# Placing two heads' sums in the last graph layer: TensorE transposes against VectorE block transposes and on-chip transfers

## The chip, the cores and the metric

The kernel runs on one core of a Trainium2 chip. A core has TensorE (PE in the profile, with its weight loads as PEld), VectorE (DVE), ScalarE (ACT), GpSimd (POOL) and SyncE (SP), which issues transfers; ACT and GpSimd can issue them too. Work in fast memory lies in SBUF (128 partitions), sums of matmuls in PSUM, and large arrays in DRAM. The metric is the device time of one execution in microseconds.

## The reference

Four graph layers follow one another on 3327 nodes with 512 features. Each is added to its input and normalised by rows. Layers 0, 2 and 3 are attention layers, layer 1 averages over the first 64 neighbours. The last layer, which the change touches, is this (4 heads of 128 features):

```python
h = (x @ W).reshape(N, HEADS, HEAD_DIM).transpose(1, 0, 2)
si = jnp.einsum('hnd,d->hn', h, a1)
sj = jnp.einsum('hnd,d->hn', h, a2)
e = si[:, :, None] + sj[:, None, :]
e = jnp.where(e > 0, e, ALPHA * e)
e = jnp.where(adj[None, :, :] > 0, e, NEG_INF)
attn = jax.nn.softmax(e, axis=-1)
h_prime = jnp.einsum('hij,hjd->hid', attn, h)
...
x = _layernorm(x + jax.nn.elu(h_prime), axis=-1)
```

## The kernel before, in words

Nodes are padded to 26 tiles of 128 (`NT`), in two halves of 13 (`HALF`, 1664 nodes, `IW`). An attention layer runs over the two halves of the receiving nodes and, within each, over four slices of 128 features (`s`; in the last layer a slice is a head). One such pass is a call of `unit`. It walks over the 26 tiles `j` of sending nodes: VectorE makes the weights `t` (L405, 128 x 1664), ACT makes `y` from them (L408), TensorE adds `t` times the features `vj` into four PSUM banks `po` (L428), and a little later adds the rows' denominators into `pd` (L380). The features come by `vj` loads on SP (L416), two tiles to a load, in four buffers; `t` has three buffers.

At the end of a unit `po` holds the head's sums with features on partitions and nodes along the row, and they have to be turned round. The kernel has two ways.

In the last layer's first half (`by_dma`), VectorE transposes each bank in 32 x 32 blocks into `ob` (L446), and four transfers on SP place the blocks in DRAM (`hd`, L473), 128 bytes for each node and block row. These rows are loaded again later as `h` (L126) for the finishing of the half: division by the denominators, ELU, residual, normalisation, store to `out`.

In the second half (`final` is given), ACT copies three banks and VectorE one into `ob` (L448, L450). TensorE then transposes 128 x 128 at a time (L456) into PSUM tiles `pt`, four at most to a tile, as background jobs in the steps of the next unit. For heads 0 and 1, `final` copies each `pt` into `g` (L1010), the tile of SBUF that holds the second half's 13 x 512 results with nodes on partitions. For heads 2 and 3 it works on `pt` directly.

Background work stands in two lists: `jobs` (transposes, and after head 1 `place`, which brings the denominators into place through GpSimd's transfers, L517, and `finish_sums`), and `aside`, made by `later`. In the second half, `aside` holds the finishing of the first half's seven groups of tiles, and then `first_slots`, which divides heads 0 and 1 in `g` (L994), applies ELU and adds the input. One job of each list is taken after each step. TensorE's order is that of the program. The other engines and the queues are put in order by a scheduler with a cost model of its own, apart from a few instructions that are pinned.

Of the kernel before, what the change touches and what calls it, by code (L numbers as in the profile page):

```python
# [18 lines left out]
P = 128  # L19
# [13 lines left out]
def kernel(  # L33
# [10 lines left out]
    nc = tc.nc  # L44
# [181 lines left out]
    class Layer:  # L226
# [137 lines left out]
        def unit(self, pools, half, s, background, aside, final=None, ending=None):  # L364
            H, D, HS = self.H, self.D, self.HS
# [73 lines left out]
            den(NT - 2, late)  # L439

            ob = sp.tile([P, IW], F32, name="ob", bufs=1)
            by_dma = HS == 1 and not final
            for c, (a_, z) in enumerate(CUTS):
                if by_dma:

# [7 lines left out]
            def transposed(s0, n):  # L453
                pt = qp.tile([P, 4, P], F32, name="pt", tag="q")
                for q in range(n):
                    nc.tensor.transpose(pt[:, q, :], ob[:, (s0 + q) * P:(s0 + q + 1) * P], ident)  # L456
                if final:
                    return final(s, s0, n, pt)
                if HS == 2 and half == 1 and s == NS - 1 and n < 4:
                    hb = vp.tile([P, n, P], F32, name="hb", tag="vj")  # L460
                elif HS == 2 and half == 1 and s == NS - 1 and s0 >= 8:
                    hb = sp.tile([P, 4, P], F32, name="hb", tag="db", bufs=1)
                else:
                    hb = sp.tile([P, 4, P], F32, name="hb")
                nc.scalar.copy(hb[:, :n], pt[:, :n])
                nc.sync.dma_start(out=hd[(t0 + s0) * P:(t0 + s0 + n) * P, s * P:(s + 1) * P]
                                  .rearrange("(t p) f -> p t f", p=P), in_=hb[:, :n])

            nothing = lambda: None
            jobs = [nothing, nothing]  # L470
            if by_dma:
                for b in range(4):
                    nc.sync.dma_start(out=hd[i0:i0 + IW, s * P + 32 * b:s * P + 32 * b + 32]  # L473
                                      .rearrange("(q i) f -> i q f", i=32),
                                      in_=ob[32 * b:32 * b + 32, :].rearrange("p (q f) -> p q f", f=32))
            else:
                for s0, n in QUADS:
                    jobs += [lambda s0=s0, n=n: transposed(s0, n), nothing]
# [413 lines left out]
    def third(first):  # L892
        with tc.tile_pool(name="col3", bufs=1) as cp, tc.tile_pool(name="at_r3", bufs=2, reuse_waits="tile") as rp:
# [52 lines left out]
            with tc.tile_pool(name="f3", bufs=2) as fp, tc.tile_pool(name="f4", bufs=1) as gp:  # L946
                g = gp.tile([P, HALF, F], F32, name="g")
# [57 lines left out]
                    return [divide, add]  # L1005

                def final(s, q0, n, pt):
                    qs = slice(q0, q0 + n)
                    if s < 2:
                        nc.vector.tensor_copy(g[:, qs, s * P:(s + 1) * P], pt[:, :n])  # L1010
                        return

                    y = g[:, qs, s * P:(s + 1) * P]
                    held = {}

                    def divide():
                        held["h"] = fp.tile([P, 4, P], F32, name="h", bufs=2) if q0 < 8 or s < NS - 1 else \
                            fp.tile([P, n, P], F32, name=f"h{q0}", bufs=1)
                        return nc.vector.tensor_tensor(held["h"][:, :n], pt[:, :n], rec[:, HALF + q0:HALF + q0 + n, s:s + 1]
                                                       .to_broadcast([P, n, P]), op=ALU.mult)  # L1020

                    def exp():
                        held["e"] = fp.tile([P, 4, P], F32, name="e") if q0 < 8 or s < NS - 1 else \
                            fp.tile([P, n, P], F32, name=f"e{q0}", bufs=1)
                        return nc.scalar.activation(held["e"][:, :n], held["h"][:, :n], AF.Exp)

                    def add1():
                        return nc.vector.scalar_tensor_tensor(y, held["e"][:, :n], 1.0, y, op0=ALU.min, op1=ALU.add)

                    def add2():  # L1030
                        return nc.vector.scalar_tensor_tensor(y, held["h"][:, :n], 0.0, y, op0=ALU.max, op1=ALU.add)

                    if s == NS - 1:
                        lasts.append((q0, n, exp, add1, add2))
                        return lambda: keep(divide())
                    divide()
                    exp()
                    add1()
                    add2()
# [3 lines left out]
                keep = tc.keep_in_program_order  # L1043
                L3.attention(rp, lambda pool, half, s: [lambda: L3.prepare(fp, 1, "xr", 2), lambda: L3.cut(fp, 1, "e", 2)]
                             if (half, s) == (0, 0) else [], later=later, final=final)

                def scale(q0, n):
# [177 lines left out]
```

## Time and profile before

| what | value |
|---|---|
| median of 4 runs | 3389.65 us (3384.63 to 3391.98) |
| the profiled execution | 3389.19 us, span 3387.5 us |
| granted clock of TensorE, mean | 0.985 |
| last layer, second half: first matmul of heads 0, 1, 2, 3 (by the timeline) | 3021.26, 3107.41, 3192.69, 3275.22 us |
| last layer, first half: first matmul of heads 1, 2, 3 | 2777.54, 2858.78, 2940.02 us |

The profile is that of one execution. Times in its views are microseconds from the start of the span, except for single durations, which are in nanoseconds where the row says so. A row names line, engine, operation and tile (`out<-in`), with the count behind an x. "Idle before" and the arrow name what ended a wait; `issue` means that the profile shows no wait. Instructions that issue transfers have a time on the queue (SPq), which is the time of the issue and not of the data. Unit 0 of each half also makes 104 small matmuls for the denominators that the other units do not.

### The profile page before, as it was taken

How to read it: one execution, taken by the hardware profiler on the slowest of the kernel's cores; microseconds unless marked ns; L12 is line 12 of the kernel's file. 1: busy time of each engine (PE TensorE's matmuls, PEld its weight loads, DVE VectorE, ACT ScalarE, POOL GpSimd, SP SyncE). 2: the span in 40 equal slices, each digit the busy share in tenths (PEclk: the TensorE clock that was granted, in tenths of full speed). 3: DMA queues.
4: the chain of work that ended last, by engine and by line, in shares of the span. 5: the costliest groups of instructions: out<-in, count | busy, mean ns of one | idle time of the engine just before them, and what ended most of it. 6: DMA issues, size and time to landing. Idle time of an engine off the chain costs nothing.

```text
span 3387.5 us, 47130 instructions
## 1 busy us (share of the span) xinstructions
PE 3246.1 (96%) x18424; PEld 1624.9 (48%) x18476; DVE 2686.0 (79%) x2619; ACT 2354.1 (69%) x2143; POOL 240.3 (7%) x389
## 2 busy tenths in 40 slices
PE   8799999999979999999999999999998999999997
PEld 7544344444434445545554444444446754445453
DVE  5799999999967544444449999999998766668887
ACT  2398998999953333333338999999997655558986
POOL 3100000000010011111110000000001000010110
PEclk9999999999999999999999999999998999999998
DMA  9544111110143333333320111111117411122311
GB/s 374 215 127 124 49 49 39 57 47 28 44 123 127 123 114 85 90 85 85 80 79 17 50 48 48 51 49 45 37 31 237 156 41 42 41 51 78 97 42 49
DMA packets 288014, 284.29 MB, mean 84 GB/s; under 512 B 107492, under 2 KB 223534, under 8 KB 287791
## 3 DMA queue, kind: packets, MB, share of 16 engines
q1 hardware_dynamic: 254063, 170.62, 16.6%
q0 software_dynamic: 28208, 102.96, 9.5%
q10 hardware_dynamic: 5520, 7.69, 0.7%
q8 instruction: 146, 2.39, 0.3%
q14 instruction: 77, 0.63, 0.1%
HBM read 212.01 MB, written 69.17 MB: 83 GB/s over the span
## 4 chain that ended last, share of the span: by engine, by line
PE 81%; DVE 5%; DMA 5%; issue 4%; ACT 4%; POOL 0%; SPq 0%; ACTq 0%; POOLq 0%; DVEq 0%
PE po L428 49%; PE acc L859 12%; PE pd L380 7%; PE pw L271 5%; DVE t L405 3%; PE pz L732 3%; PE pi L735 3%; DMA raw<-in_adjT_dram 2%; ACT y L408 2%; PE pk L819 1%; PE pt L456 1%; DMA h<-hd 1%; PE pa L1108 0%; PE pt L724 0%; PE pct L664 0%
## 5 line engine op out<-in xcount | busy, mean ns | idle before, releaser
L405 DVE SCALAR_TENSOR_TENSOR t<-rb,qc,mask 128x1664 f32<-128x1664 f32 x1040 | 1959.7, 1945 | 168.7 <-PE po L428 146.5
L408 ACT ACTIVATE y<-t,bi,sc 128x1664 fp8e4<-128x1664 f32 x1040 | 1769.2, 1765 | 309.6 <-PE pd L380 292.0
L428 PE MATMUL po<-t,vj 128*64 128x448 f32 (+3 forms) x8320 | 1908.4, 520 | 22.2 <-DVE t L405 19.6
L428 PEld LDWEIGHTS po<-t,vj 128*64 128x64 f32 (+1 forms) x8320 | 839.8, 148 | 968.8 <-issue 701.8
L859 PE MATMUL acc<-zs,kt 128*128 128x512 bf16 x1312 | 394.6, 382 | 2.4 <-issue 0.4
L271 PE MATMUL pw<-wsb,xT 128*128 128x264 f32 (+1 forms) x1248 | 297.6, 393 | 17.1 <-DVE vt L277 13.5
L859 PEld LDWEIGHTS <-kt 128*128 128x128 fp8e4 x2002 | 196.7, 98 | 243.1 <-issue 10.0
L811 ACT CAST pk<-cy 128x512 f32<-128x512 bf16 x169 | 99.0, 588 | 279.5 <-DVE kt L823 269.0
L380 PE MATMUL pd<-y,sden 128*32 128x448 fp8e4 (+1 forms) x4160 | 259.5, 341 | 10.4 <-ACT y L408 10.4
L271 PEld LDWEIGHTS pw<-wsb,xT 128*128 128x128 f32 x1248 | 237.8, 194 | 61.7 <-ACT xT L262 10.0
L859 PE MATMUL acc<-zl,kt 128*128 128x512 bf16 x638 | 242.1, 379 | 0.6
L380 PEld LDWEIGHTS <-sden 128*32 128x32 bf16 x4160 | 117.5, 96 | 162.5 <-issue 139.8
L823 DVE SCALAR_TENSOR_TENSOR kt<-pk,mask 128x512 fp8e4<-128x512 f32 x169 | 116.1, 687 | 96.1 <-PE pk L819 96.1
L277 DVE TENSOR_TENSOR vt<-pw,dc 128x256 f32<-128x256 f32 x156 | 58.9, 418 | 146.9 <-ACT dc L272 143.7
L359 POOL DMA_DIRECT2D rb<-r x40 | 21.3, 534 | 1670.8 <-DVE t L405 1653.1
L275 ACT COPY rc<-pw 128x8 f32<-128x8 f32 (+1 forms) x78 | 12.7, 163 | 156.4 <-PE pw L271 156.4
L732 PE MATMUL pz<-wn,xT 128*128 128x512 f32 x208 | 94.6, 598 | 1.7 <-ACT xT L726 1.7
L831 DVE SCALAR_TENSOR_TENSOR y<-acc,cnt,bnb 128x512 f32<-128x512 f32 x26 | 19.5, 750 | 96.6 <-PE acc L859 89.2
L700 POOL DMA_DIRECT2D cy<-ctd x91 | 68.1, 748 | 386.0 <-ACT pk L811 313.4
L735 PE MATMUL pi<-wl,xT 128*128 128x512 f32 x208 | 93.5, 592 | 0.0
L634 DVE TENSOR_SCALAR mask<-raw 128x832 fp8e4<-128x832 int32 (+2 forms) x90 | 54.0, 608 | 40.1 <-DMA raw<-in_adjT_dram 39.5
L154 ACT ACT_TABLE_LOAD x45 | 57.7, 1283 | 37.0 <-DVE mv L153 36.4
(187 smaller groups left out, 1699.2 us busy)
## 6 DMA issues: line engine op xcount, KB each, us to landing
vj<-v SPq DMA_DIRECT2D x312, 128.0 KB
rb<-r POOLq DMA_DIRECT2D x40, 832.0 KB, 4.6
raw<-in_adjT_dram SPq DMA_DIRECT2D x67, 416.0 KB
cy<-ctd POOLq DMA_DIRECT2D x78, 256.0 KB, 3.9
h<-hd SPq DMA_DIRECT2D x61, 256.0 KB
v<-vt SPq DMA_DIRECT2D x50, 256.0 KB
hd<-hb SPq DMA_DIRECT2D x48, 256.0 KB
xr<-x POOLq DMA_DIRECT2D x45, 256.0 KB, 3.1
```

The costliest lines, as they stand in the source:

```text
L271: nc.tensor.matmul(pw[e][:, :FW + H], xT[:, c, :], wsb[:, c, e, :], start=c == 0, stop=c == FC - 1)
L277: nc.vector.tensor_tensor(vt[:, hs, :], pw[e][:, :FW].rearrange("p (h d) -> p h d", d=D), self.dc[:, t, hs].rearrange("p (h e) -> p h e", e=1)
L380: nc.tensor.matmul(pd[c][32 * kk:32 * kk + 32, :w_], lhsT, rhs, start=(kk, c) not in seen, skip_group_check=final is not None, stop=last a ...
L405: nc.vector.scalar_tensor_tensor(t, rb[k], self.qc[:, j, h:h + 1], mask[:, j, i0:i0 + IW], op0=ALU.max, op1=ALU.mult)
L408: nc.scalar.activation(y, t, AF.Sigmoid, bias=self.bi[:, j, h:h + 1], scale=self.sc[:, j, h:h + 1], saturate=False)
L428: nc.tensor.matmul(po[c][k * D:(k + 1) * D, :z - a_], vj[:, j % 2, k * D:(k + 1) * D], ts[k][:, a_:z], start=j == 0, stop=j == NT - 1)
L700: nc.gpsimd.dma_start(out=cy[:, :n, :], in_=ctd[t:t + n, b * GW:(b + 1) * GW] .rearrange("(o t) i -> o t i", o=1).to_broadcast([P, n, GW]))
L732: nc.tensor.matmul(pz, xT[:, c, :], wn[:, c, :], start=c == 0, stop=c == FC - 1)
L735: nc.tensor.matmul(pi, xT[:, c, :], wl[:, c, :], start=c == 0, stop=c == FC - 1)
L811: nc.scalar.copy(pks[k % 2], carry[b, t // 4 * 4][:, t % 4:t % 4 + 2, :])
L823: nc.vector.scalar_tensor_tensor(kt, pk, NEIGHBOURS, mask[:, t:t + 2, i0:i0 + GW], op0=ALU.is_le, op1=ALU.mult, saturate=False)
L859: nc.tensor.matmul(acc, kts[t][:, s * P:(s + 1) * P], zs(t, c) if c < 2 else zl[:, t, :], start=t == 0 and c == 0, stop=t == NT - 1 and c ...
```

## The change

For heads 0 and 1 of the second half the first half's way is taken up to `ob`: VectorE transposes the four banks in 32 x 32 blocks. Sixteen transfers on SP for each head then go from `ob` to `g`, both in SBUF: for each of four block rows `b` of 32 features, and each of four residues `m` of the node's block number, the 32 partitions of `b` go to the 32 partitions of `m`, in 13 x 32 blocks of 32 floats. TensorE's transposes of these two heads, their copies to `ob` on ACT and VectorE, and the copies from `pt` to `g` are gone. Heads 2 and 3 stay as they are.

```diff
-            by_dma = HS == 1 and not final
+            by_dma = HS == 1 and (not final or s < 2)
...
-            if by_dma:
+            if by_dma and final:
+                for b in range(4):
+                    for m in range(4):
+                        final(s, b, m, ob[32 * b:32 * b + 32, :].rearrange("p (q m f) -> p q m f", m=4, f=32)[:, :, m, :])
+            elif by_dma:
...
                 def final(s, q0, n, pt):
+                    if s < 2:
+
+                        nc.sync.dma_start(out=g[32 * n:32 * n + 32, :, s * P + 32 * q0:s * P + 32 * q0 + 32], in_=pt)
+                        return
                     qs = slice(q0, q0 + n)
-                    if s < 2:
-                        nc.vector.tensor_copy(g[:, qs, s * P:(s + 1) * P], pt[:, :n])
-                        return
```

## The prediction

> **What bounds the kernel now.** I read the busy shares first, then cut the last layer into its eight units (two halves of four heads) at the first `po` matmul of each, then asked what each cut waits for, then what stands at the two places where the change works.
>
> The page's busy shares, and then the busy time in three windows: the unit of head 2 in the first half, and the units of heads 1 and 2 in the second (columns: window, its length, busy time of each engine with its count). A unit's window holds the transposes of the head before it, because `ob` is worked off in the background of the next unit.
>
> ```profile
> PE 3246.1 (96%) x18424; PEld 1624.9 (48%) x18476; DVE 2686.0 (79%) x2619; ACT 2354.1 (69%) x2143; POOL 240.3 (7%) x389
> ```
> ```profile
> 2858.78:2940.02 81.24, 81.24 (x314) 40.25 (x313) 52.64 (x32) 44.72 (x27) 0.53 (x1) 1.00 0.17 43
> 3107.41:3192.69 85.28, 83.28 (x327) 41.47 (x325) 73.62 (x78) 78.27 (x63) 5.05 (x9) 1.00 0.29 95
> 3192.69:3275.22 82.53, 82.53 (x328) 41.49 (x326) 72.38 (x78) 74.98 (x61) 13.73 (x23) 1.00 0.19 56
> ```
>
> TensorE never rests in the first line, which is a unit of the first half, where VectorE transposes and transfers already do what the change brings to the second half. In the second line (it holds head 0's transposes) PE rests 2.00 us, in the third (head 1's) not at all. The waits inside the second line's window:
>
> ```profile
> PE pd L380 <- ACT y L408: 1.8, 1, 1.8
> PE po L428 <- DVE t L405: 0.2, 1, 0.2
> ```
>
> The operations on `ob` over the whole run, by tile. L446 and L473 are the first half's way, L456 with L448, L450 the second's, and the copies to `g` are L1010:
>
> ```profile
> L446 DVE STREAM_TRANSPOSE ob<-po x16: 539/572/643, 2775.2 to 3021.2; 128x448 f32<-128x448 f32 x8, 128x384 f32<-128x384 f32 x8
> L473 SPq DMA_DIRECT2D hd<-ob x16: 321/1094/1861, 2777.3 to 3024.6; - x16
> L450 DVE COPY ob<-po x4: 606/621/625, 3105.3 to 3354.9; 128x448 f32<-128x448 f32 x4
> ```
> ```profile
> L1010 DVE COPY g<-pt x8: 278/682/693, 3120.3 to 3228.0; 128x512 f32<-128x512 f32 x6, 128x128 f32<-128x128 f32 x2
> ```
>
> The chain of waits across the boundary between heads 0 and 1:
>
> ```profile
> 3103.91 5.37 DMA h<-hd
> 3109.99 1.28 DVE t L405
> 3114.72 1.95 DVE t L405
> 3116.72 3.06 PE po L428 x8
> ```
>
> A load of `h` for the finishing of the first half heads VectorE's queue there, and PE's 0.22 us wait shows that nothing is left between it and PE. VectorE at the next boundary, heads 1 to 2:
>
> ```profile
> 3187.79 0.61 DVE L450 COPY ob<-po 128x448 f32<-128x448 f32 x1
> ...
> 3192.51 1.94 DVE L405 SCALAR_TENSOR_TENSOR t<-rb,qc,mask 128x1664 f32<-128x1664 f32 x1
> ...
> 3196.89 1.95 DVE L405 SCALAR_TENSOR_TENSOR t<-rb,qc,mask 128x1664 f32<-128x1664 f32 x1
> ```
>
> VectorE is busy back to back from 3183.9 to 3201.9. PE starts head 2 at 3192.69, needs its third `t` after 16 of 32 matmuls that together take 11.44 us, at about 3198.4, and that `t` ends at 3198.84. So VectorE, too, has no slack in these few microseconds, though it rests 10 to 12 us over the whole unit.
>
> **The change, part by part.**
>
> 1. *PE loses 26 transposes (L456, 13 for each of heads 0 and 1).* Against the first-half unit, the window of head 1's transposes is 82.53 - 81.24 = 1.29 us longer, that of head 0's 85.28 - 81.24 - 2.00 of rest = 2.04. Ends: 2 x 1.29 = 2.6 and 3.3. I take 3.3, what the windows say. It is PE time on the path: -3.3.
> A rule of the Trainium skill speaks against the move: "VectorE: DVE Perf Modes", sections The three transpose paths and Rules for kernel authors, sends a 128x128 transpose to TensorE, as VectorE transposes only 32x32 blocks, and states 390 ns for TensorE's. The windows here give about 0.10 us a transpose, hidden in the pipeline among matmuls; 26 at the page's figure would be an estimate of 10.1 us, and the time about 3380. I go by the windows.
>
> 2. *ACT loses six `ob` copies (L448, about 0.48 us: 2.9 us).* Three were at 3104.8 to 3106.4, before an idle of 2.97 us on the load of `h`: nothing gained. Three were at 3192.1, after the late `y` that PE waits 1.78 us for. That `y` is late since two table swaps stand before it on ACT, and their order is the scheduler's, which plans anew with the lighter load. Ends: no stall goes, or both (2.0 us). I take half: -1.0.
>
> 3. *VectorE: four transposes (L446) in place of one copy (L450), per head.* Four took 2.10 us in a row at 2775.17 against 0.62: +1.48. At the first boundary VectorE idles from 3105.9 to 3109.4, which covers it: 0. (Were that cover gone, +1.5 us.) At the second there is no cover, and PE's third `t` waits one for one: ends 0, if the scheduler puts other work behind it, and 1.48 plus the waits on the old transfers that read `ob` (six event instructions of 49 ns stand at L446 in the first half: 0.3), 1.8. I take +1.5, as the window shows full occupation. The eight copies to `g` (6 x 0.68 + 2 x 0.28 = 4.6 us) also go, but at 3120 to 3135 and 3207 to 3228, where PE does not wait: 0.
>
> 4. *SP: 32 more transfers, 16 after each head, each of 32 x 13 blocks of 128 bytes.* They wait for all four transposes. Behind them on SP stand `vj` loads, `h` loads, `out` stores and, for head 1, `dd`. No transfer within SBUF is in the trace; issue costs between L473's shortest 0.32 us and GpSimd's 0.59 for the 16 small `pes` transfers (L517, 9.36 us from first to last): 5.1 to 9.4 us of SP. I take 0.36, SP's own for a `vj`: 5.8. The data: head by head the first half moves the same 6656 blocks of 128 bytes, and the queue was so filled for 7 us:
>
> ```profile
> DMA packets 7077, 1.02 MB, mean 133 GB/s; under 512 B 6740, under 2 KB 7077, under 8 KB 7077
> q1 hardware_dynamic: 7077, 1.02, 82.7%
> ```
>
> (2777.3 to 2785; 0.827 x 16 x 7.7 us / 7077 = 14.4 ns a packet.) A `vj` is loaded three pairs of steps ahead, 3 x 81.24 / 13 = 18.7 us, and even one after the other 9.4 of issue, 7 of data and 2 of landing (an estimate: the `vj` issued at 2783.43 keeps the queue busy until about 2785.4) make 18.4: hidden by that cover, which is nearly used up in this worst order. In the first half issue and data overlap (the four L473 take 4.6 of the 7 us) and no unit waits. And for head 1 the first use of `g` (L994, 3217.5) is 25 us after the transposes. I take 0, by the first half, the nearest row; ends 0 and +12.7 (the second rival).
> On the Trainium skill: "DMA: Bandwidth & Descriptors", section Specifications, says that transfers under 512 bytes cost a read, modify and write, which speaks against 128-byte blocks, while its section Why small descriptors are slow (HBM only) exempts SBUF to SBUF; no row here shows such a transfer. Taken as a doubling of the 7 us, an estimate, the first gives 14 + 2 us, still under 18.7, and by either section the sum stays at -2.8.
>
> 5. *Order.* `place` and `finish_sums` keep their third and ninth job after head 1. VectorE's first L994 now waits for transfers; behind it stand `t`s, but 25 us covers it. Without that, each microsecond late would be one of PE.
>
> Sum: -3.3 - 1.0 + 1.5 + 0 = -2.8 us. The profiled execution took 3389.19 (span 3387.5 and 1.7 around it), 0.46 under the median of the runs; so 3386.4, and 3386.9 as a median, say 3387.
>
> **The rivals.** 0.2% is 6.8 us, about what a measurement of this kernel can tell from no change: faster is under 3382.9, slower over 3396.4.
>
> *All stalls go as well:* -3.3 - 2.0 = -5.3, 3384.3. For it: ACT is lighter. Against: VectorE sits next in line at the second boundary. As the four runs shown spread over 7.4 us, such a case can also read under 3382.9.
>
> *SP holds back the `h` load (slower).* Place: the boundary of heads 0 and 1. If the transfers, ready at about 3107.4, stand before the `h` load of 3103.91 on SP, that load starts at 3107.4 + 5.8 to 9.4 = 3113.2 to 3116.8, and lands 9.3 to 12.9 us later than now; VectorE's queue is headed by its user and PE has 0.22 us to spare, so 9.1 to 12.7 pass through: 3396 to 3400. It decides from 9.5 us of delay on. For it: in the program the transfers come before that load. Against: the load is ready earlier, and the scheduler puts a ready one ahead.
>
> *Blocks move slowly within SBUF.* From 18.7 - 2 = 16.7 us / 416 blocks an engine = 40 ns a block on, `vj` comes late. At 68 ns (the `pes` packets of 384 bytes, far off) 28 us, so 11.6 late, twice: 3410. Against: 14.4 ns in the first half, where no unit waits.
>
> *Nothing gained:* the transposes on VectorE stall both boundaries, 2 x 1.8, against 3.3: 3390.
>
> **How the numbers follow.** Forecast 0.36; all stalls go 0.24, of which 0.10 reads as faster; the `h` load 0.22, of which 0.20 slower; slow blocks 0.08; nothing gained 0.10. So faster 0.10, same 0.62, slower 0.28. The range 3381 to 3400 leaves out slow blocks, and the tails of the first two rivals; the forecast's own is 3384 to 3391.
>
> **What would show it.** Right: no L456 in the windows of heads 1 and 2, these 1.3 to 2 us nearer 81.24; eight L446 more; 32 transfers of about 0.36 us on SP; `vj` never named in a wait of PE. Wrong: a wait of PE for `vj` or for `t` behind an `h` load near 3110; L994 waiting for a transfer to `g`; a third `t` of head 2 later than PE by more than 2 us; 128-byte packets of over 40 ns.

## The result and the profile after

The changed kernel took 3395.3 us in the median against 3390.27 for the kernel before, a ratio of 1.0016 with a 95% interval of 1.0012 to 1.0021: 5 us slower, within the 0.2% that the prediction drew its line at and within its range, but to the other side than the 2.8 us of gain that it forecast.

The windows of the units of heads 1 and 2 of the second half, in the profile after (columns as before: window, its length, busy time of each engine):

```profile
3104.80:3187.52 82.72, 81.64 (x314) 40.20 (x312) 70.01 (x70) 78.14 (x62) 4.62 (x9) 1.00 0.36 105
3187.52:3276.72 89.20, 82.45 (x312) 40.20 (x312) 73.33 (x81) 78.09 (x62) 14.14 (x24) 0.98 0.25 66
```

The first window fell from 85.28 to 82.72, the second rose from 82.53 to 89.20. From the start of head 1's unit to the end of the span it is 286.0 us (3104.80 to 3390.8) against 280.1 (3107.41 to 3387.5): +5.9, of which -2.56 in head 1's unit, +6.67 in head 2's, and +1.8 behind it. All four waits of TensorE in the two units stand in its timeline (the bracket holds the wait and what ended it):

```profile
3186.87 0.54 PE L380 MATMUL pd<-y,sden 128*32 128x448 fp8e4 x6 [0.96 <-ACT y L408]
3195.47 5.85 PE L428 MATMUL po<-t,vj 128*128 128x448 f32 x16 [2.09 <-DVE t L405]
3264.70 5.85 PE L428 MATMUL po<-t,vj 128*128 128x448 f32 x16 [0.16 <-DVE t L405]
3275.89 0.90 PE L380 MATMUL pd<-y,sden 128*32 128x448 fp8e4 x6 [4.46 <-ACT y L408]
```

The 4.46 us at the end of head 2's unit are most of the loss; nothing like it was there before. ACT in that unit, one pair of `y` early in it and the last part:

```profile
3222.01 3.44 ACT L408 ACTIVATE y<-t,bi,sc 128x1664 fp8e4<-128x1664 f32 x2
...
3250.96 1.28 ACT L1001 ACT_TABLE_LOAD   x1
3252.25 0.63 ACT L1001 ACTIVATE e<-g 128x512 f32<-128x512 f32 x1
3252.90 1.28 ACT L408 ACT_TABLE_LOAD   x1
3254.19 3.44 ACT L408 ACTIVATE y<-t,bi,sc 128x1664 fp8e4<-128x1664 f32 x2
...
3271.04 1.28 ACT L1001 ACT_TABLE_LOAD   x1
3272.34 0.42 ACT L1001 ACTIVATE e<-g 128x256 f32<-128x256 f32 x1
3272.77 1.28 ACT L408 ACT_TABLE_LOAD   x1
3274.07 1.77 ACT L408 ACTIVATE y<-t,bi,sc 128x1664 fp8e4<-128x1664 f32 x1
```

`e<-g` is the exponential in the ELU of heads 0 and 1. It needs another table than `y`, so each one costs two loads here. With two `y` a pair of steps so takes 6.69 us of ACT (3252.90 to 3259.59, the next load of the same kind), and TensorE wants one each 6.27 us, so ACT falls behind by 0.4 us a pair. Two loads for the normalisation's `rs` (3225.47 and 3227.08), and the two that stand before the last, single `y`, cost it more. From the end of the `y` of 3222.01 to the end of the last one (3275.84) ACT makes 14 `y` in 50.4 us, where TensorE takes 43.9. Of these 6.5 us, 4.46 come out as TensorE's wait; the rest must have been ACT's slack. Before, the same work on ACT began 12.5 us earlier in the unit and was over three pairs before its end. One load also served three of the seven exponentials, so that ACT loaded a table 16 times in the unit, and 20 times after the change. The end of the unit before:

```profile
3255.13 1.28 ACT L997 ACT_TABLE_LOAD   x1
3256.43 0.42 ACT L997 ACTIVATE e<-g 128x256 f32<-128x256 f32 x1
3256.86 1.28 ACT L408 ACT_TABLE_LOAD   x1
3258.16 3.44 ACT L408 ACTIVATE y<-t,bi,sc 128x1664 fp8e4<-128x1664 f32 x2
3262.41 3.44 ACT L408 ACTIVATE y<-t,bi,sc 128x1664 fp8e4<-128x1664 f32 x2 [0.81 <-PE pd L380]
3268.68 3.44 ACT L408 ACTIVATE y<-t,bi,sc 128x1664 fp8e4<-128x1664 f32 x2 [2.83 <-PE pd L380]
```

The waits for `pd` in the last two lines are ACT's slack, which the kernel after has not. Its SP queue across the boundary of heads 1 and 2:

```profile
3188.96 11.69 SPq L1014 DMA_DIRECT2D g<-ob  x16
3200.76 0.53 SPq L511 DMA_DIRECT2D dd<-red  x1
3202.71 1.09 SPq L133 DMA_DIRECT2D out_dram<-h  x2
```

The denominators `dd`, ready since the sums of 3191.95 to 3192.9, go out at 3200.76, behind the sixteen transfers: 13.2 us into the unit, where it was 7.1 before (3199.76). The ELU needs them. And the new operations on `ob` by tile:

```profile
L1014 SPq DMA_DIRECT2D g<-ob x32: 591/621/1734, 3106.9 to 3200.0; - x32
L446 DVE STREAM_TRANSPOSE ob<-po x24: 536/572/650, 2772.6 to 3188.4; 128x448 f32<-128x448 f32 x12, 128x384 f32<-128x384 f32 x12
```

A transfer costs SP 0.62 us in the median, where 0.36 was taken.

### The profile page after: what moved, and what is told of

The parts are those of the page before. It is cut to its first block, busy times and chain, and to the rows that moved or that the text cites. A ratio compares the mean times of both kernels' runs of the same rounds, so it can differ in the third digit from the quotient of the medians.

```text
span 3390.8 us, 47126 instructions
## 1 busy us (share of the span) xinstructions
PE 3249.5 (96%) x18398; PEld 1627.6 (48%) x18450; DVE 2685.9 (79%) x2617; ACT 2357.4 (70%) x2141; POOL 240.0 (7%) x389
## 4 chain that ended last, share of the span: by engine, by line
PE 82%; DVE 5%; issue 5%; DMA 4%; ACT 3%; POOL 0%; SPq 0%; ACTq 0%; POOLq 0%; DVEq 0%
PE po L428 49%; PE acc L863 12%; PE pd L380 7%; PE pw L271 5%; DVE t L405 3%; PE pz L736 3%; PE pi L739 3%; DMA raw<-in_adjT_dram 2%; ACT y L408 1%; PE pk L823 1%; PE pt L456 1%; DMA h<-hd 0%; PE pa L1113 0%; PE pt L728 0%; PE pct L668 0%
```

## The experiments

The theory after the result: the transfers hold up the chain from the denominators to the ELU of heads 0 and 1; its exponentials stand later in ACT's order, and their table loads run into the end of head 2's unit. Each kernel's median and ratio below are against runs of the kernel before on the same chip. An interval that holds 1 does not tell a kernel from the one before; those that do so here end at 1.0008 or less, below the 1.0012 at which the full change's begins.

### One head at a time

```diff
-            by_dma = HS == 1 and (not final or s < 2)
+            by_dma = HS == 1 and (not final or s == 0)
...
```

> Only head 0 is placed by block transposes and transfers; head 1 goes by TensorE as before. Theory (head 1's transfers hold the denominators back on SP, the ELU of the first two heads starts late and ACT's table swaps run into the end of head 2's unit): the window of head 1 keeps its 82.7 us instead of 85.3, head 2's unit stays near 82.5, so about 2.6 us below before, 3387.7. Rival (sixteen transfers on SP cost TensorE time by themselves, wherever they stand): no gain or a loss, 3390 to 3393.

Measured: 3387.88 against 3390.44, ratio 0.9991 (0.9983 to 1.0000). Head 1's unit took 82.70 us, 2.6 below before, and head 2's 83.50, 1.0 above, with 0.70 of waiting for `t` at its start and none at its end. So head 0's way is worth 2.6 us in its own window and 1.6 over the two units, and its sixteen transfers stand in no wait of TensorE. The interval touches 1, so the runs alone hardly show the gain.

With `s == 1` in place of `s == 0`:

> Only head 1 is placed by block transposes and transfers; head 0 goes by TensorE as before. Theory: head 1's window stays at 85.3 us, head 2's unit grows to about 89 and its late end drops TensorE's clock once more, so 6.7 + 1.8 us above before, about 3398.8, slower than the full change. Rival (the loss needs both heads' transfers): within 2 us of before, 3390.

Measured: 3395.62 against 3390.44, ratio 1.0016 (1.0007 to 1.0024). Head 2's unit took 88.53 us and its end has the same wait of 4.46. So it is head 1's way that brings the loss. TensorE does not wait for `t` at the start of this unit; instead its first 32 matmuls take 13.13 us there, 11.44 before. The loss is 3 us less than expected in the median, though from the start of head 1's unit to the end of the span the trace is 7.7 us over before; the profiled execution (span 3395.2) was no outlier, and what the median lacks was not found.

### The denominators on another queue

```diff
-                nc.sync.dma_start(out=dd, in_=red...)
+                (nc.gpsimd if final and s == 1 else nc.sync).dma_start(out=dd, in_=red...)
```

> The full change, with head 1's denominators sent to DRAM by GpSimd's queue instead of SP's, where they stood behind the sixteen transfers. Theory: the ELU of the first two heads starts 5 to 8 us earlier in head 2's unit, ACT's wait of 4.5 us at its end and the clock drop of 1.9 us behind it shrink or go: 3389 to 3391. Rival (the ELU is late because the transfers into g are): unchanged, 3395.

Measured: 3389.53 against 3390.44, ratio 0.9999 (0.9990 to 1.0008). The transfers are as in the full change, and yet the wait at the end is 0.23 us and head 2's unit 84.17. The first `e<-g` starts 32.2 us into the unit (44.6 in the full change, 32.1 before). It is the denominators, and not the data in `g`, that the start of the ELU was late for. The last `e<-g` still stands at 80.2 us, against 63.7 before; what spreads them is not shown.

### The tables

```diff
-                        nc.scalar.activation(e[:, :n], y, AF.Exp)
+                        nc.scalar.activation(e[:, :n], y, AF.Sigmoid, saturate=False)
```

> The full change, with the exponential in the ELU of heads 0 and 1 (second half) replaced by a sigmoid, which is in the table that ACT has loaded, so that fourteen table loads are gone; this part of the result is another. Theory: the 4.5 us wait of TensorE for ACT at the end of head 2's unit and the 1.9 us of clock behind it go, 2.1 us of VectorE at its start stay: 3389. Rival (ACT's tables don't matter, VectorE or the transfers do): 3395.

Measured: 3388.41 against 3390.44, ratio 0.9995 (0.9986 to 1.0004). TensorE's waits in the two units:

```profile
PE po L428 <- DVE t L405: 2.1, 1, 2.1
PE pd L380 <- ACT y L408: 1.0, 1, 1.0
```

The first `e<-g` is about as late as in the full change (43.2 us into the unit), but the wait at the end is gone. With no loads between them the seven also lie closer together, and the last is at 63.9 us (84.8 in the full change). A late start without the table loads costs nothing; the two make the loss together.

### The transfers behind the denominators

```diff
+                def blocks(b):
+                    for m in range(4):
+                        final(s, b, m, ...)
+                if s == 1:
+                    jobs += [lambda b=b: blocks(b) for b in range(4)]
...
```

> The full change, but head 1's sixteen transfers are issued as background jobs of head 2's unit, four after a step, behind the denominators. Theory (the transfers' place on SP ahead of the denominators is the loss): the ELU of the first two heads starts early enough for ACT to be done before the unit's end, the 4.5 us wait and the clock drop are gone, the 2.1 us wait for VectorE at the unit's start stays: head 2's unit about 83.4 us, 3388.5 in all. Rival (the data must be in g early): ELU late, 3395.

Measured: 3389.47 against 3391.51, ratio 0.9995 (0.9986 to 1.0004). Head 2's unit took 83.59 us, with the 2.08 us at its start alone. `dd` goes out at 3196.9, between the third and the fourth transfer; the others follow over 15 us, and nobody waits for them.

### Fewer issues, over DRAM

```diff
+                for b in range(4):
+                    nc.sync.dma_start(out=hd[i0:i0 + IW, s * P + 32 * b:s * P + 32 * b + 32]..., in_=ob[32 * b:32 * b + 32, :]...)
+                final(s, 0, 0, hd[i0:i0 + IW, s * P:(s + 1) * P]...)
...
-                        nc.sync.dma_start(out=g[32 * n:32 * n + 32, ...], in_=pt)
+                        nc.gpsimd.dma_start(out=g[:, :, s * P:(s + 1) * P], in_=pt)
```

> The full change, but the blocks go to DRAM in four transfers of SP for each head, as in the first half, and come back in one load of GpSimd. Theory that SP's time for sixteen issues (about 11 us against 4.6) is the price: the denominators come 6 us earlier than in the full change, 3389 to 3391. Rival (the ELU waits for whatever comes last, and the way over DRAM is as long): the wait at the end of head 2's unit stays, 3393 to 3396.

Measured: 3397.73 against 3391.51, ratio 1.0016 (1.0007 to 1.0025): the rival. The wait at the end is 4.47 us. SP is free sooner, and `dd` goes out 6.9 us into the unit (3200.39, unit from 3193.45), about as early as before. But GpSimd's load of `g` now stands ahead of `place`:

```profile
3204.42 1.19 POOL L1016 DMA_DIRECT2D g<-hd  x1 [5.28 <-DMA dd<-red]
3205.61 4.18 POOL L523 DMA_DIRECT2D pes<-dd  x7
3211.09 5.11 POOL L523 DMA_DIRECT2D pes<-dd  x9 [1.29 <-DMA g<-hd]
```

The profile puts the wait of 5.28 us to the landing of `dd`, and only the 1.29 to the load of `g`. `place` starts 12.2 us into the unit, 2.9 later than before. So the number of issues on SP is not what decides. Nor can this small delay be: the last kernel of this section starts `place` at the same 12.2 us and has no wait at the end. What is late is the ELU's place in ACT's order (first `e<-g` at 44.6 us, as in the full change).

### All transfers on GpSimd

```diff
-                        nc.sync.dma_start(out=g[32 * n:32 * n + 32, ...], in_=pt)
+                        nc.gpsimd.dma_start(out=g[32 * n:32 * n + 32, ...], in_=pt)
```

> The full change with all 32 transfers issued by GpSimd. Theory (what counts is when the denominators are in place, and GpSimd places them): they stand behind 16 x 0.6 us on GpSimd instead of SP, so little is won, 3392 to 3395. Rival (only SP's queue with its loads and stores matters): 3389.

Measured: 3390.46 against 3391.51, ratio 0.9996 (0.9987 to 1.0004), between the two. `dd` goes out 5.4 us into the unit, `place` starts at 13.3 behind 16 transfers of 0.64 us, the first `e<-g` is 40.0 us into the unit, and the wait at the end 1.96. More was won than the theory said.

### Each transfer cut in two

```diff
+                        for a_, z in ((0, 7), (7, HALF)):
+                            nc.sync.dma_start(out=g[32 * n:32 * n + 32, a_:z, ...], in_=pt[:, a_:z, :])
```

> The full change with each transfer cut in two (7 and 6 of its 13 columns of blocks), 32 for a head; ACT's order of instructions is the same as in the full change. If a transfer costs SP a fixed 0.6 us, SP is held about 20 us for a head, else about 11 as before. Theory that the planned order of ACT's work is the loss, not SP's time: the wait at the end of head 2's unit stays 4.5 us and the time 3395 to 3396 even if SP is held twice as long. Rival (SP's time itself delays what TensorE needs): denominators or features later, 3400 or more.

Measured: 3399.26 against 3390.69, ratio 1.0027 (1.0017 to 1.0038), between the two statements and nearer to the rival's. SP's row, and TensorE's waits:

```profile
L1015 SPq DMA_DIRECT2D g<-ob x64: 586/606/999, 3109.3 to 3213.6; - x64
```
```profile
3132.74 5.83 PE L428 MATMUL po<-t,vj 128*128 128x448 f32 x16 [1.30 <-DMA vj<-v]
3191.10 0.54 PE L380 MATMUL pd<-y,sden 128*32 128x448 fp8e4 x6 [1.30 <-ACT y L408]
3192.29 5.86 PE L428 MATMUL po<-t,vj 128*128 128x448 f32 x16 [0.66 <-DVE ob L446]
3200.24 7.55 PE L428 MATMUL po<-t,vj 128*128 128x448 f32 x16 [2.09 <-DVE t L405]
3271.16 5.85 PE L428 MATMUL po<-t,vj 128*128 128x448 f32 x16 [0.16 <-DVE t L405]
3282.35 0.54 PE L380 MATMUL pd<-y,sden 128*32 128x448 fp8e4 x6 [4.47 <-ACT y L408]
```

Half the blocks cost the same 0.6 us, so the price is by the transfer. SP is held 20.8 us, and now `vj` does come late, by 1.30. The two units together take 3.9 us more than in the full change: this wait, 0.66 for `ob`, 0.34 more for `y` in head 1's unit, and two slow stretches of matmuls (7.55 and 6.24 us for 5.85). So far the rival holds, and SP's time does cost TensorE when it is doubled. The denominators leave 22.1 us into the unit (3214.35), 8.8 later than in the full change, and the wait at the end is the same to 0.01 us. It is thus not the time at which the denominators arrive that sets it, but the place of the ELU in ACT's order, which is the same in the two kernels: the scheduler had planned it late enough for both.

### The wait at the start of head 2's unit

In the kernel with the denominators on GpSimd's queue, VectorE's transposes and sums for them become the first background job:

```diff
-                for c in range(2):
-                    ins = nc.vector.transpose(db[:64, ...], pd[c][:64, ...])
...
+                def gather():
+                    ...
+                if final and s == 1:
+                    jobs[0] = gather
```

> As the kernel with head 1's denominators on GpSimd's queue (3389.5 measured), and VectorE's four transposes and two sums of the denominators become the first background job of head 2's unit. Theory (these stand ahead of the third weight tile and make TensorE's 2.1 us wait at the start): that wait goes, 3387.4. Rival (the denominators, later by some microseconds, bring ACT's late end back): 3391 or more.

Measured: 3390.90 against 3391.51, ratio 0.9996 (0.9987 to 1.0005), and the wait is still 2.08 us. The scheduler put the same instructions in the same order on VectorE as without the edit, so this tells nothing of either theory.

Then `gather` as the third job, its first transpose pinned behind the weight tile that TensorE waited for, and the transfers behind it as in the kernel of the background jobs:

```diff
+                        if (end or final and s == 1) and c == 0:
+                            tc.keep_in_program_order(ins)
...
-                return jobs[:2] + [place] + jobs[2:7] + [finish_sums] + jobs[7:]
+                return jobs[:2] + ([gather] if final and s == 1 else []) + [place] + jobs[2:7] + [finish_sums] + jobs[7:]
```

> Both heads by blocks, head 1's transfers as background jobs as in the kernel bg, and VectorE's transposes of the denominators pinned behind the third weight tile of head 2's unit. Theory (each wait has its own cause and both can be taken away): the 2.1 us wait at the start and the 4.5 us wait at the end are gone, head 2's unit about 81.5 us, 2 us under bg, 3386 to 3387.5, faster than before by about 0.1%. Rival (VectorE's queue only moves the wait to another tile, or ACT's late end comes back with the later denominators): 3389 or more.

Measured: 3387.44 against 3390.69, ratio 0.9988 (0.9979 to 0.9996): faster than both kernels. Its two windows and what TensorE waits for in them:

```profile
3108.23:3190.96 82.73, 81.65 (x315) 40.21 (x313) 70.08 (x71) 78.15 (x62) 4.63 (x9) 1.00 0.37 104
3190.96:3273.51 82.55, 82.04 (x313) 40.00 (x313) 72.62 (x81) 74.87 (x60) 14.14 (x24) 1.00 0.27 69
```
```profile
PE pd L380 <- ACT y L408: 1.0, 1, 1.0
PE po L428 <- DVE t L405: 0.5, 2, 0.4
```

The third `t` now starts 2.6 us after TensorE began the unit (3193.53) where it was 6.0 (3193.48 in the full change, unit from 3187.52), and TensorE no longer waits for it. The 0.35 us that are left come after 24 matmuls, at 3199.96, and are for the fourth `t`, which now stands behind the denominators' transposes: a small part of the 2.1 us was moved to another tile, as the rival has it. Head 2's unit is 1.0 us below that of the background jobs, not the 2 expected. 0.5 us of waits are left, and TensorE's busy time is 0.5 us longer (82.04 against 81.50): sixteen matmuls take 6.12 us for 5.85 from 3247.35 on, and the next sixteen as much, in two parts. Why is not known.

### All kernels side by side

Times within head 2's unit, in us from its first `po` matmul: `place` is the first of its transfers, `e` the ELU's exponential. Loads are ACT's table loads in the unit, and the wait is TensorE's last for `y`.

| kernel | `place` | first `e` | last `e` | loads | wait, us | unit, us |
|---|---|---|---|---|---|---|
| before | 9.3 | 32.1 | 63.7 | 16 | none | 82.53 |
| the change | 15.7 | 44.6 | 84.8 | 20 | 4.46 | 89.20 |
| head 1 alone | 13.9 | 44.0 | 84.1 | 20 | 4.46 | 88.53 |
| over DRAM | 12.2 | 44.6 | 84.8 | 20 | 4.47 | 89.19 |
| transfers cut in two | 24.6 | 46.3 | 86.5 | 20 | 4.47 | 90.53 |
| transfers on GpSimd | 13.3 | 40.0 | 81.9 | 20 | 1.96 | 85.89 |
| denominators on GpSimd | 8.6 | 32.2 | 80.2 | 17 | 0.23 | 84.17 |
| the same, sums as a job | 8.3 | 32.2 | 80.1 | 17 | 0.23 | 84.15 |
| head 0 alone | 6.3 | 37.7 | 75.4 | 18 | none | 83.50 |
| background jobs | 7.7 | 34.6 | 72.6 | 17 | none | 83.59 |
| background jobs, pinned | 12.2 | 32.8 | 70.9 | 17 | none | 82.55 |
| sigmoid for the exponential | 16.0 | 43.2 | 63.9 | 6 | none | 83.60 |

The wait goes with the last `e`, behind which a load and the unit's last `y` stand in the kernels that have it: none up to 75 us into the unit, 0.23 at 80.2, 1.96 at 81.9, 4.46 at 84.8. It does not go with the start of `place`. The five kernels with 20 loads are also the five with a long wait; more loads make the last `e` later, and no run changes the number of loads at a fixed last `e`.

## Why the prediction was wrong

*Step 1, TensorE's transposes, -3.3.* Right in kind. In head 1's unit TensorE's time without waits fell from 83.28 to 82.72 - 0.96 = 81.76, in head 2's from 82.53 to 83.59 - 2.08 = 81.51 (background jobs): -2.5 together, just under the lower end of 2.6, or 0.10 us a transpose. By the 390 ns that the prediction quotes from the Trainium skill, "VectorE: DVE Perf Modes", The three transpose paths, the 26 would make an estimated 10.1 us; the measurement is far from it.

*Step 2, ACT's copies, -1.0.* The two waits of 2.00 us became one of 0.96. The half that was taken is what came, but it was the middle between two ends and not worked out from the order on ACT: the number is luck.

*Step 3, VectorE, +1.5.* The place was right, the reason not. The prediction read the `t` that ended at 3198.84 as head 2's third, with no slack. It was the fourth: before, 32 matmuls ran 11.44 us from 3192.69 without a wait, 2.86 us a tile, so TensorE wanted the third `t` at 3198.4, and it had been ready since 3194.45; the fourth was wanted at 3201.3. VectorE had 4.0 and 2.4 us to spare. After the change the third `t` is late by 2.09 us all the same, just over the 2 us that the prediction named as a sign of being wrong, because the scheduler moved other work of VectorE ahead of it: normalisation, and the transposes and sums of the denominators. With head 0 alone, so with a copy and no transposes at that boundary, it is 0.70, so the transposes are 1.39 of it. That this is near 1.5 is luck. At the first boundary VectorE's idle time covered the transposes, as said.

*Step 4, SP.* A transfer was sized at 0.36 us and measured 0.62; sixteen took 10.7 to 11.7 us, over the upper end of 9.4. Even so `vj` is in no wait of TensorE, and the rival of the `h` load did not come: that load was issued at 3101.03, ahead of the transfers at 3106.88. Slow blocks fell as well. Between 3188 and 3204 us of the profile after:

```profile
DMA packets 7295, 1.67 MB, mean 104 GB/s; under 512 B 6960, under 2 KB 7088, under 8 KB 7294
q1 hardware_dynamic: 7135, 1.13, 41.7%
```

That is 0.417 x 16 x 16 us / 7135 = 15.0 ns a packet, within SBUF about as to DRAM (14.4). (The 68 ns at which the prediction priced slow blocks does not come out of its row either: 0.159 x 16 x 12 us over the 537 packets of GpSimd's queue is 57 ns.) On the Trainium skill, "DMA: Bandwidth & Descriptors": against the first half's packets, the doubling that was weighed for transfers below 512 bytes (Specifications) does not show, and no gain within SBUF (Why small descriptors are slow) either. Both rows have blocks of 128 bytes, so what small blocks cost against large ones is not shown by them.

*Step 5, order.* This is the step that failed. It kept `place` and `finish_sums` at their places in the list of jobs and took 25 us as cover for the first use of `g`. VectorE indeed never waited for `g`. But the list is only the program's order; the scheduler plans the other engines' order, and step 4 had itself named `dd` as standing behind the transfers on SP. With the transfers ahead of the denominators, their use and the whole ELU behind it came 12.5 us later in the unit, though the denominators themselves went out only 6 us later. The prediction looked for a wait of the first user (L998, from 3226.2). The price came 45 us after that on another engine: ACT had its slack at the end of the unit, and lost it, and TensorE stood still for 4.46 us from 3271.4. With the denominators on GpSimd's queue and nothing else changed, the wait is 0.23 us.

Of the 5.9 us in the profiled executions, steps 1 to 3 make -2.5 - 1.0 + 2.1 = -1.4. The late `y` is 4.5 and the slower clock behind it 1.9; and the unit's last sixteen `pd` matmuls, split by the wait, took 0.94 and 0.90 us, where they took 0.94 in one piece before: another 0.9. The term that stood for all this was the 0 of step 4.

That the scheduler's own estimate of the transfers moved the ELU is argued from its orders (moving the denominators or the transfers moves it back, while the time at which `place` starts does not decide) and not seen directly.

## What to carry to other kernels

Where a scheduler orders the engines, look for what stands behind an added transfer in its queue, and follow that to its last user: a late consumer may cost nothing where it stands and much where its work ends up. An engine whose work swaps tables has a slack that is used up pair by pair; ask at which step it was over before, and not whether the engine is busy. Queue the transfers that nobody needs soon behind those whose results feed such work.

## What the runs showed of the hardware

A transfer within SBUF on SP, of 32 partitions and 13 or 6 and 7 blocks of 128 bytes each, takes 0.59 us of issue at least, at either size; a `vj` load takes 0.36, and the shortest of the first half's transfers to DRAM, with 52 blocks a partition, 0.32.

The wait of 4.46 us also slowed what followed. The first 32 matmuls of head 3's unit, after the change and before it:

```profile
3276.72 13.36 PE L428 MATMUL po<-t,vj 128*128 128x448 f32 x32
```
```profile
3275.22 11.44 PE L428 MATMUL po<-t,vj 128*128 128x448 f32 x32
```

That is 1.92 us more, at a granted clock of 0.85 (1.00 before). The same 32 took 13.66, 12.62 and 13.09 us in the other three kernels with that wait, and 11.44 in those with 1.96, 0.23 or none. The Trainium skill, "TensorE: Matmul & The Clock Gate", Part 1: The HAM clock gate, has the clock halved after an idle window of about 3.4 us, and these rows agree. But the kernel with the transfers cut in two also shows 16 matmuls of 7.55 us for 5.85 behind a wait of only 2.09 (3200.24 above), with 0.66 and 1.30 shortly ahead of it. And with head 1 alone the 32 matmuls of 13.13 us, at a clock of 0.87, stand behind a wait of 1.78 us, the same that the kernel before has ahead of 11.44 us at 1.00. Shorter waits can cost a slow stretch too, and do not always.
